# Written order, half-row loads and a bounded softmax around the attention stages of a four-layer kernel

## Chip, cores and metric

The kernel runs on one core of a Trainium2 chip as one launch. The metric is the time of one execution on the device in microseconds (us), lower is better. Three runs of the kernel before gave 7562.25, 7568.02 and 7576.92 us, with a median of 7568.02 us. About 0.2% (15 us) is the smallest difference that such runs can tell from none.

## What is computed

The reference takes 8 images of 56 x 56 places with 128 channels through four layers, all in float32. Layers 0 (a deformable convolution) and 1 (a whitening of channels) are not touched. Layers 2 and 3, on the 3136 tokens t of an image, are

```python
# layer 2
h = (layernorm(t) @ W_k.T) in 8 heads of 16
t = t + softmax(h h.T / 4) h @ W_o.T          # h is query, key and value
t = t + experts(layernorm(t))
# layer 3
q, k, v = (layernorm(t) @ w_in.T) in 4 heads of 32
q = softmax(q over the 32 of a head) / sqrt(32)
k = softmax(k over all 3136 tokens)
t = t + layernorm(((k.T v / 3136) applied to q) @ w_out.T + b_out) * ln_w
t = t + experts(layernorm(t))
```

`experts` takes the logits of 64 experts for every token and a softmax over the tokens; each expert takes its 8 best tokens of an image, sums them with their weights, passes the sum through a two-layer network, and adds the result back to those tokens.

## The kernel before

Layer 2 begins in `attention_keys` (L1038), image by image. Two loads bring the image (`y` in device memory) as the tile `t`, 112 tokens on the partitions and 28 groups on the free axis; 28 pairs of `bn_stats` and `bn_aggr` on DVE (L1066, L1067) give mean and variance; `rsqrt` (L1135) takes the power -1/2 of all 28 at once on POOL (L1140); 28 normalisations on DVE write `xn` (in `normalize`, L112); TensorE transposes each (L121) and ACT copies four at a time to `xT` (L122). From `xT` come the keys, 14 products `p_h` of 448 columns (L1082), whose results go to `kT` by turns on DVE (L1090) and ACT (L1086), and the values, 25 pairs `p_v` (L1097), copied to `va` by turns on ACT (L1105) and DVE (L1107). `kT` and `va` are stored to device memory. POOL squares the image's `va` (L1116), DVE sums the squares by head (L1118) and takes the largest (L1119). After the last image a bound `low` of all scores follows from that. In this function the order of instructions on each engine is chosen when the kernel is built, by a scheduler that follows the program's order where it has no reason to leave it. `query_bound` (L2079) then takes a bound `low3` of layer 3's queries from the rows of `w_in`, with a flag `small3` that is 1 while the bound is below 40.

`attend` (L1154) is the main part: for each image, half of its heads and block of up to 384 queries (9 blocks) it makes scores (L1251), takes exponentials (L1259) and multiplies by the values (L1304). A finished block is divided, projected (L1374) and added to its tokens (L1385), normalised (L1390 to L1399), transposed (L1411) and given its expert logits `pr` (L1415, L1416). These finishing steps are a generator that `later` holds; at the end of the program two of those that are left go on at a time. The last image's choice of tokens (`choose`, L1654: largest 8, L1659; their places, L1662; gathers, L1726; exponentials, L1693; sum, L1721) follows.

`context_sums` (L1947) is the first part of layer 3. Of each of 56 groups of 448 tokens it takes statistics (L2018, L2019), power (L1140), `ms` (L2026), normalisation on ACT (L2033), transposition to `xT`, which is stored too, and the keys `p_k` with channels on the partitions (L1980). As the softmax over tokens needs a bound that is not known, it carries a running maximum: DVE takes each group's maximum (L1983, L1985), ACT the exponential with it (L1992) and the factor `fall` by which the earlier sums shrink (L1987); the exponentials are transposed (L1997), copied (L1998), multiplied with the tokens (L2002), and DVE adds to `tot` and `den` (L2004, L2005). `linear_layer` (L2106) is the second part. A group passes ten steps, one per turn of `pipeline` (L1934), which starts a group each turn and lets every group in flight go one step, oldest first: load `xT`; `p_q` (L2131) and exponential (L2144); sum, reciprocal, `q*m` on POOL (L2148); transposition of q; `p_y` (L2155), squares on ACT (L2161), `rs` (L2165, L2166); `y` on DVE (L2169) and `t = t + y` on POOL (L2172); statistics; `ms` and `xn`, with two stores of t (L2181); transposition; `p_g` (L2187) and `pr` (L2188). After an image's seventh group `choose` follows in the same turns. Here too the scheduler decides the order in the end. Groups hold three buffers of most tiles, and images two of `t`.

Of the kernel before, what the change touches and what calls it, by code (L numbers as in the profile page):

```python
# [8 lines left out]
F32 = mybir.dt.float32  # L9
I32 = mybir.dt.int32  # L10
# [1027 lines left out]
def attention_keys(tc, k, w, yv, tok, kT_out, va_out, low, small):  # L1038
# [5 lines left out]
    n_b = yv.shape[1]  # L1044
    with ExitStack() as ctx:
        cp = ctx.enter_context(tc.tile_pool(name="akc", bufs=1))
        bp = ctx.enter_context(tc.tile_pool(name="akb", bufs=2))
        ps = ctx.enter_context(tc.tile_pool(name="akp", bufs=6, space=PSUM))
        vas = []
# [8 lines left out]
        for n in range(n_b):  # L1058
            t_sb = bp.tile([T, NT, C], F32, name="t")
            for h in range(2):  # L1060
                nc.sync.dma_start(t_sb[h * IW : (h + 1) * IW], yv[h, n])
            nc.sync.dma_start(tok[n].rearrange("(t p) c -> p t c", p=T), t_sb)
# [53 lines left out]
            nc.gpsimd.tensor_tensor(sq, v, v, ALU.mult)  # L1116
            top = bp.tile([128, 2 * KT * 4], F32, name="top")
            nc.vector.tensor_reduce(top, sq, AX.X, ALU.add)  # L1118
            nc.vector.tensor_reduce(tops[:, n : n + 1], top, AX.X, ALU.max)  # L1119
# [1267 lines left out]
```

## Time and profile before

| what | us |
|---|---|
| median of three runs | 7568.02 |
| the profiled execution, its time | 7568.32 |
| its span | 7566.5 |
| layers 0 and 1, and the weights of layers 2 and 3 | to 1520 |
| `attention_keys` and `query_bound` | 1520.06 to 1867.6 |
| `attend`, main part | 1868.9 to 6411 |
| `attend`, last blocks | 6411 to 6455.0 |
| last choice, experts of layer 2 | 6455.0 to 6663.6 |
| `context_sums` | 6670.0 to 6909 |
| `context_weights` | to 6915.0 |
| `linear_layer`, first `p_q` to last `p_g` | 6926.7 to 7323.7 |
| last choice, experts of layer 3 | 7323.7 to 7566.5 |

The profiled execution took 1.8 us more than its span, and 0.3 us more than the median of the runs. The rows are read off the timeline: the first and last instruction of each function's lines. A line of the timeline has the start, the duration, the engine, the line of the kernel, the operation, what it writes and reads with shapes, how many were merged, and in brackets the idle time ahead of it with what ended it. PE is the matrix unit, PEld its weight loads, DVE the vector engine, ACT the scalar engine, POOL GpSimd, and SP the engine that starts the transfers.

### The profile page before, as it was taken

What the parts mean: (1) busy time and instruction counts of PE and PEld (TensorE: products, weight loads), DVE (VectorE), ACT (ScalarE), POOL (GpSimd) and SP (SyncE); (2) the same over time, 40 slices, a digit from 0 to 9 for tenths busy, and PEclk for the clock granted to TensorE, in tenths of its full rate; (3) what the DMA queues carried; (4) which work ended last, traced back from release to release, by engine and by line L of the source; (5) the groups of instructions that cost most, each with busy time, mean ns of one, the idle gap of its engine ahead of it and who ended that gap; (6) DMA issues with size and microseconds to landing.
All of it is one profiled execution on the core that took longest, in us unless ns stands there. A gap on an engine that the chain in (4) does not pass through costs nothing. (4 is left out here: it accounts for less than half of the span.)

```text
span 7566.5 us, 158564 instructions
## 1 busy us (share of the span) xinstructions
PE 6499.5 (86%) x60063; PEld 2893.4 (38%) x60063; DVE 5210.3 (69%) x9787; ACT 4198.0 (55%) x6563; POOL 2941.4 (39%) x2557
## 2 busy tenths in 40 slices
PE   7859999656999999999999999999999999556764
PEld 5646666433333323323323323323333323245542
DVE  7866664366677777777777777777777777356761
ACT  5634444222766666666666666666666665156750
POOL 0011111122544444444444444444444444333763
PEclk9968989866999999999999999999999999789776
DMA  6544343476888778778778778778778777544544
GB/s 162 163 101 88 85 87 63 155 224 202 198 202 205 188 187 205 190 185 205 192 186 205 189 185 206 187 189 205 191 186 206 187 185 170 202 109 125 134 132 139
DMA packets 737876, 1287.44 MB, mean 170 GB/s; under 512 B 119042, under 2 KB 504452, under 8 KB 730308
## 3 DMA queue, kind: packets, MB, share of 16 engines
q1 hardware_dynamic: 726868, 1260.77, 65.9%
q0 software_dynamic: 6144, 12.60, 0.6%
q8 instruction: 486, 7.96, 0.5%
q10 hardware_dynamic: 4080, 3.68, 0.2%
q14 instruction: 298, 2.44, 0.1%
HBM read 286.04 MB, written 197.81 MB: 64 GB/s over the span
## 5 line engine op out<-in xcount | busy, mean ns | idle before, releaser
L1259 ACT ACTIVATE e<-p_s 128x768 f32<-128x768 f32 (+2 forms) x3712 | 2887.7, 830 | 1577.2 <-PE p_s L1251 1312.7
L1297 POOL COPY x<-sq 32x1152 f32<-32x1152 f32 x1792 | 2062.4, 1151 | 2008.8 <-PE p_s L1251 1240.1
L1270 DVE STREAM_TRANSPOSE sq<-e 128x768 f32<-128x768 f32 x2688 | 2433.8, 950 | 516.7 <-ACT e L1259 267.0
L1251 PE MATMUL p_s<-q,kT 32*128 32x384 f32 (+2 forms) x14848 | 1893.4, 547 | 41.1 <-ACT e L1259 23.3
L1304 PE MATMUL av<-e,va 128*32 128x384 f32 (+2 forms) x14848 | 1644.2, 515 | 13.5 <-DVE acc L1327 8.5
L1304 PE MATMUL avx<-x,va 128*32 128x384 f32 x10752 | 1129.5, 492 | 57.5 <-issue 36.9
L1251 PEld LDWEIGHTS p_s<-q,kT 32*128 32x128 f32 (+1 forms) x14848 | 649.9, 180 | 1265.8 <-issue 836.1
L1304 PEld LDWEIGHTS av<-e,va 128*32 128x32 f32 (+1 forms) x14848 | 293.6, 108 | 1028.7 <-issue 938.6
L1304 PEld LDWEIGHTS avx<-x,va 128*32 128x32 f32 x10752 | 351.8, 111 | 635.8 <-issue 597.4
L616 POOL TENSOR_TENSOR rs<-rs,mhalf 112x4 f32<-112x4 f32 x112 | 116.0, 1036 | 786.2 <-DVE rs L615 786.2
L1323 DVE TENSOR_TENSOR acc<-acc,avx 128x384 f32<-128x384 f32 x336 | 183.7, 547 | 232.3 <-PE avx L1304 227.7
L121 PE MATMUL p_tr<-ident,xn 112*128 112x112 f32 x672 | 132.9, 337 | 184.0 <-DVE xn L112 138.3
L1140 POOL TENSOR_TENSOR rs<-rs,mhalf 112x4 f32<-112x4 f32 (+2 forms) x136 | 167.9, 1235 | 243.6 <-DVE ntop L1985 123.9
L532 ACT COPY wT<-p_w 88x448 f32<-88x448 f32 x152 | 138.1, 923 | 197.8 <-PE p_w L530 159.4
L2033 ACT ACTIVATE xn<-t,ms,rs 112x128 f32<-112x128 f32 x448 | 185.2, 487 | 73.8 <-DVE ms L2026 73.7
L644 PE MATMUL p_f<-x1T,w 128*128 128x448 f32 x448 | 206.1, 584 | 4.4 <-DVE x1T L639 2.8
L121 PEld LDWEIGHTS p_tr<-ident,xn 112*128 112x128 f32 x672 | 97.3, 167 | 278.2 <-issue 184.9
L530 PE MATMUL p_w<-ident,wide 112*88 112x112 f32 x896 | 144.6, 300 | 62.7 <-DMA px<-strips 37.8
L1393 POOL TENSOR_TENSOR rs_b<-rs_b,mhalf 128x3 f32<-128x3 f32 (+1 forms) x72 | 58.5, 815 | 352.8 <-DVE rs_b L1392 350.2
L327 DVE SCALAR_TENSOR_TENSOR acc<-xp,dw,acc 128x3136 f32<-128x3136 f32 x48 | 166.5, 3470 | 37.6 <-ACT acc L322 37.3
L628 DVE TENSOR_TENSOR y<-y,p_rs 128x448 f32<-128x448 f32 x112 | 69.2, 618 | 176.7 <-PE p_rs L621 176.6
L122 ACT COPY xT<-p_tr 128x448 f32<-128x448 f32 x112 | 59.6, 532 | 224.8 <-PE p_tr L121 198.7
(366 smaller groups left out, 7904.0 us busy)
## 6 DMA issues: line engine op xcount, KB each, us to landing
x<-sq SPq DMA_DIRECT2D x5376, 144.0 KB
w<-in_L_ffn_weight_dram SPq DMA_DIRECT2D x64, 1024.0 KB
px<-strips SPq DMA_DIRECT2D x64, 616.0 KB
va_d<-va SPq DMA_DIRECT2D x16, 1600.0 KB
xT_d<-xT SPq DMA_DIRECT2D x112, 224.0 KB
xT<-xT_d SPq DMA_DIRECT2D x112, 224.0 KB
kT_d<-kT SPq DMA_DIRECT2D x16, 1568.0 KB
t<-t_a SPq DMA_DIRECT2D x16, 1568.0 KB
```

The source lines that it names most:

```text
L121: nc.tensor.transpose(p[:, i, :], src[:, i, :], k.ident[:T, :T])
L327: nc.vector.scalar_tensor_tensor(acc, xp[:, j // 3 : j // 3 + IH, j % 3 : j % 3 + IW], dw[:, j : j + 1], acc, ALU.mult, ALU.add,)
L530: nc.tensor.transpose(p[:, g], around[:, :, g], k.ident[:T, :T])
L644: nc.tensor.matmul(p, q.w1[:, f * 128 : (f + 1) * 128], x1T, start=True, stop=True)
L1140: nc.gpsimd.tensor_tensor(rs, rs, k.mhalf[:m, :n], ALU.pow)
L1251: nc.tensor.matmul(ss[j // 2][:m, j % 2, :width], kT[rows, 128 * i : 128 * i + m], q[rows, :width], start=True, stop=True,)
L1259: nc.scalar.activation(e[:m, 2 * j : 2 * j + 2, :width], ss[j][:m, :, :width], AF.Exp)
L1270: nc.vector.transpose(sq[:, :, i, j : j + 2].rearrange("p s j c -> p j s c"), exps[u, b, a, i][:, j : j + 2, :QB].rearrange("p j (s c) -> ...
L1297: nc.gpsimd.tensor_copy(*moves.pop(0))
L1304: nc.tensor.matmul(out, keys[u, b][1][:m, i, j, :], e[j], start=start, stop=stop)
L1323: nc.vector.tensor_tensor(to, to, in_order(av), ALU.add)
L2033: nc.scalar.activation(out[:, i], x[:, i], AF.Identity, bias=ms[:, i : i + 1], scale=rs[:, i : i + 1])
```

## The change

In five places:

- `attention_keys` runs under `manual_schedule`: each engine gets its instructions in the order in which the program writes them. The loads of an image are taken by half rows, so that a partition reads 28 tokens that lie together (14336 bytes) where it read single tokens of 512 bytes; the token stores are alike. The tokens of a transposed group are then 28 apart, and ACT's copy puts them in place with a stride. Statistics and power of image n+1 are written between the key products of image n. All 14 key results go through ACT. The square of image n stays on POOL after its values, and DVE's two reductions of it come after the normalisation of image n+1.
- The last blocks of `attend` all go on together, from before the last jobs, with their `t` and `xT` in two buffers that the exponentials no longer need.
- `query_bound` becomes `score_bound`: it takes the rows of keys too, and stands at the head of the token layers.
- `context_sums_bounded` is new and is taken where `small3` is 1, `context_sums` otherwise. It has no maximum and no rescaling: `low3` stands in for the maximum, the keys come out with tokens on the partitions, so that the exponentials need no transposition, and one accumulator in PSUM runs over all 56 groups; a column of ones beside the tokens gives the denominator. It is under `manual_schedule`.
- `linear_layer` is under `manual_schedule`, with no operation changed.

```diff
-def attention_keys(tc, k, w, yv, tok, kT_out, va_out, low, small):
+def attention_keys(tc, k, w, y, tok, kT_out, va_out, low, small):
...
+        ctx.enter_context(
+            tc.manual_schedule(
+                engines={
+                    e.engine for e in (nc.tensor, nc.scalar, nc.vector, nc.gpsimd, nc.sync)
+                }
+            )
+        )
...
+        def statistics(n):
...
             t_sb = bp.tile([T, NT, C], F32, name="t")
-            for h in range(2):
-                nc.sync.dma_start(t_sb[h * IW : (h + 1) * IW], yv[h, n])
-            nc.sync.dma_start(tok[n].rearrange("(t p) c -> p t c", p=T), t_sb)
+            inner = tok[n].rearrange("(h f i) c -> f h i c", f=2, i=NT)
+            for f in range(2):
+                of = slice(f * IH, (f + 1) * IH)
+                nc.sync.dma_start(t_sb[of], y[:, n, f * NT : (f + 1) * NT])
+            yield
+            for f in range(2):
+                nc.sync.dma_start(inner[f], t_sb[f * IH : (f + 1) * IH])
             mv = bp.tile([T, NT, 2], F32, name="mv")
             st = bp.tile([T, NT, 6], F32, name="st")
             for i in range(NT):
                 nc.vector.bn_stats(st[:, i], t_sb[:, i])
                 nc.vector.bn_aggr(mv[:, i], st[:, i])
-            rs = rsqrt(nc, k, bp, mv, NT)
+                if i % GT == GT - 1:
+                    yield
+            stats[n] = t_sb, mv, rsqrt(nc, k, bp, mv, NT)
...
+        def largest(n):
...
+            sq = bp.tile([128, 2 * KT * 4, DK], F32, name="sq", bufs=1)
+            v = vas[n % 2].rearrange("p g t j d -> p (g t j) d")[:, :, :DK]
+            nc.gpsimd.tensor_tensor(sq, v, v, ALU.mult)
+            yield
+            top = bp.tile([128, 2 * KT * 4], F32, name="top")
+            nc.vector.tensor_reduce(top, sq, AX.X, ALU.add)
+            nc.vector.tensor_reduce(tops[:, n : n + 1], top, AX.X, ALU.max)
+        stats, tail = {}, []
+        ahead = [statistics(0)]
+        while ahead:
+            advance(ahead)
+        for n in range(n_b):
+            t_sb, mv, rs = stats.pop(n)
+            if n + 1 < n_b:
+                ahead.append(statistics(n + 1))
+                advance(ahead)
             xT = bp.tile([C, S], F32, name="xT")
+            by_place = xT.rearrange("c (h f i) -> c i f h", f=2, i=NT)
             for g in range(NG):
                 xn = bp.tile([T, GT, C], F32, name="xn")
                 for i in range(GT):
                     normalize(nc, xn[:, i], t_sb[:, g * GT + i], mv, rs, g * GT + i)
-                transpose_group(
-                    nc, k, ps, "m", xT[:, g * QC : (g + 1) * QC], xn, nc.scalar.copy
-                )
-            kT = bp.tile([128, 2, S], F32, name="kT", bufs=1)
+                p = ps.tile([C, GT, 2, IH], F32, tag="m", name="p_tr")
+                for i in range(GT):
+                    nc.tensor.transpose(
+                        p[:, i].rearrange("c f h -> c (f h)"), xn[:, i], k.ident[:T, :T]
+                    )
+                nc.scalar.copy(by_place[:, g * GT : (g + 1) * GT], p)
+            advance(tail)
+            kT = bp.tile([128, 2, S], F32, name="kT")
             for g in range(2):
...
                         p, wk[:, g * 128 : (g + 1) * 128], xT[:, cols], start=True, stop=True
                     )
-                    if c % 2:
-                        nc.scalar.activation(
-                            kT[:, g, cols], p, AF.Identity, bias=w.one16, scale=DK**-0.25
-                        )
-                    else:
-                        nc.vector.tensor_scalar(
-                            kT[:, g, cols], p, DK**-0.25, w.one16, ALU.mult, ALU.add
-                        )
+                    advance(ahead)
+                    nc.scalar.activation(
+                        kT[:, g, cols], p, AF.Identity, bias=w.one16, scale=DK**-0.25
+                    )
                 nc.sync.dma_start(kT_out[n, g], kT[:, g])
+            assert not ahead
             va = vas[n % 2]
             for t, m in key_tiles():
                 p = ps.tile([128, 2, 4, DK], F32, tag="m", name="p_v")
@@ -1107,16 +1148,10 @@
                     nc.vector.tensor_copy(va[:m, :, t, :, :DK], p[:m])
             for g in range(2):
                 nc.sync.dma_start(va_out[n, g], va[:, g].rearrange("p t j d -> p (t j d)"))
-            sq = bp.tile([128, 2 * KT * 4, DK], F32, name="sq", bufs=1)
-            v = va.rearrange("p g t j d -> p (g t j) d")[:, :, :DK]
-            nc.gpsimd.tensor_tensor(sq, v, v, ALU.mult)
-            top = bp.tile([128, 2 * KT * 4], F32, name="top")
-            nc.vector.tensor_reduce(top, sq, AX.X, ALU.add)
-            nc.vector.tensor_reduce(tops[:, n : n + 1], top, AX.X, ALU.max)
+            tail.append(largest(n))
+            advance(tail)
+        while tail:
+            advance(tail)
...
-            t_sb = wp.tile([128, KB + 1, C], F32, name="t", bufs=2)
+            if ending:
+                t_sb = rooms[0].pop().rearrange("p (a c) -> p a c", c=C)
+            else:
+                t_sb = wp.tile([128, KB + 1, C], F32, name="t", bufs=2)
...
-            st = wp.tile([128, KB + 1, 6], F32, name="st", bufs=2)
-            mv = wp.tile([128, KB + 1, 2], F32, name="mv", bufs=2)
-            rs = wp.tile([128, KB + 1], F32, name="rs_b", bufs=2)
+            st = wp.tile([128, KB + 1, 6], F32, name="st", bufs=NQ)
+            mv = wp.tile([128, KB + 1, 2], F32, name="mv", bufs=NQ)
+            rs = wp.tile([128, KB + 1], F32, name="rs_b", bufs=NQ)
...
-            xT = wp.tile([C, QB + 64], F32, name="xT", bufs=2)
+            if len(rooms) == 2:
+                xT = rooms[1].pop()
+            else:
+                xT = wp.tile([C, QB + 64], F32, name="xT", bufs=2)
...
+        def room():
+            flat = tp.tile([128, 4, KB, 4, KB * 32], F32, name="sq")
+            flat = flat.rearrange("p s a j c -> p (s a j c)")
+            return [flat[:, 512 * i : 512 * i + 512] for i in range(NQ)]
...
+        def go_on_all():
...
+        ending = True
+        rooms = [room()]
+        early = 3
         while jobs:
             keep_squares()
+            if early:
+                go_on_all()
+                early -= 1
             from_squares()
-        for work in urgent:
-            go_on(work)
-        ending = True
+            while urgent:
+                go_on(urgent.pop(0))
+        while urgent:
+            go_on(urgent.pop(0))
+        rooms.append(room())
         while later:
-            for work in later[:2]:
-                go_on(work)
+            go_on_all()
...
+def context_sums_bounded(tc, k, w, low, t_in, xT_out, tot, den):
...
+        bp = ctx.enter_context(tc.tile_pool(name="cbb", bufs=3))
+        wp = ctx.enter_context(tc.tile_pool(name="cbw", bufs=3))
+        ps = ctx.enter_context(tc.tile_pool(name="cbp", bufs=7, space=PSUM))
+        pa = ctx.enter_context(tc.tile_pool(name="cba", bufs=1, space=PSUM))
...
+        sums = pa.tile([C, C + 1], F32, name="sums")
...
+        def load():
...
+        def group(n, g):
+            if g == 0:
+                load()
...
+            rs, mv = group_stats(nc, k, wp, t)
+            yield
+            ms = minus_mean(nc, wp, rs, mv)
+            xn = wp.tile([T, GT, C + 1], F32, name="xn", bufs=6)
+            nc.gpsimd.memset(xn[:, :, C:], 1.0)
+            for i in range(GT):
+                if i % 2:
+                    nc.scalar.activation(
+                        xn[:, i, :C],
+                        t[:, i],
+                        AF.Identity,
+                        bias=ms[:, i : i + 1],
+                        scale=rs[:, i : i + 1],
+                    )
+                else:
+                    nc.vector.tensor_scalar(
+                        xn[:, i, :C],
+                        t[:, i],
+                        rs[:, i : i + 1],
+                        ms[:, i : i + 1],
+                        ALU.mult,
+                        ALU.add,
+                    )
+            yield
+            p = ps.tile([C, GT, T], F32, tag="m", name="p_tr")
+            for i in range(GT):
+                nc.tensor.transpose(p[:, i], xn[:, i, :C], k.ident[:T, :T])
+            xT = wp.tile([C, QC], F32, name="xT")
+            nc.scalar.copy(xT, p.rearrange("c a t -> c (a t)"))
+            nc.sync.dma_start(xT_out[n][:, g * QC : (g + 1) * QC], xT)
+            yield
+            p = ps.tile([T, GT, C], F32, tag="m", name="p_k")
+            for i in range(GT):
+                nc.tensor.matmul(
+                    p[:, i],
+                    xT[:, i * T : (i + 1) * T],
+                    w.w_in[:, C : 2 * C],
+                    start=True,
+                    stop=True,
+                )
+            e = wp.tile([T, GT, C], F32, name="e")
+            nc.scalar.activation(e, p, AF.Exp, bias=low[:T])
+            yield
+            for i in range(GT):
+                nc.tensor.matmul(
+                    sums,
+                    e[:, i],
+                    xn[:, i],
+                    start=(n == 0 and g == 0 and i == 0),
+                    stop=(n == n_b - 1 and g == NG - 1 and i == GT - 1),
+                )
+        load()
+        load()
+        pipeline([group(n, g) for n in range(n_b) for g in range(NG)], 1)
+        nc.vector.tensor_copy(tot, sums[:, :C])
+        nc.vector.tensor_copy(den, sums[:, C:])
...
-def query_bound(tc, k, w, w_in, low, small):
+def score_bound(tc, k, w_in, low, small):
...
-        raw = bp.tile([C, C], F32, name="raw")
-        nc.sync.dma_start(raw, w_in[:C])
-        sq = bp.tile([C, C], F32, name="sq")
+        raw = bp.tile([C, 2, C], F32, name="raw")
+        nc.sync.dma_start(raw, w_in[: 2 * C].rearrange("(a p) c -> p a c", p=C))
+        sq = bp.tile([C, 2, C], F32, name="sq")
         nc.vector.tensor_tensor(sq, raw, raw, ALU.mult)
+        norms = bp.tile([C, 2], F32, name="norms")
+        nc.vector.tensor_reduce(norms, sq, AX.X, ALU.add)
         norm = bp.tile([C, 1], F32, name="norm")
-        nc.vector.tensor_reduce(norm, sq, AX.X, ALU.add)
+        nc.vector.tensor_reduce(norm, norms, AX.X, ALU.max)
...
         bp = ctx.enter_context(tc.tile_pool(name="llb", bufs=2))
         wp = ctx.enter_context(tc.tile_pool(name="llw", bufs=3))
...
+        ctx.enter_context(
+            tc.manual_schedule(
+                engines={
+                    e.engine for e in (nc.tensor, nc.scalar, nc.vector, nc.gpsimd, nc.sync)
+                }
+            )
+        )
...
+        low3 = cp.tile([128, 1], F32, name="low3")
+        small3 = cp.tile([1, 1], I32, name="small3")
+        score_bound(tc, k, a["L3_attn_w_in"], low3, small3)
...
+            attention_keys(tc, k, w, y, tok, kT_d, va_d, low, small)
...
-        low3 = cp.tile([128, 1], F32, name="low3")
-        small3 = cp.tile([1, 1], I32, name="small3")
-        query_bound(tc, k, w, a["L3_attn_w_in"], low3, small3)
...
-        context_sums(tc, k, w, t_a, xT_d, tot, den)
+        sums = (t_a, xT_d, tot, den)
+        taken = nc.values_load(small3[0:1, 0:1], min_val=0, max_val=1)
+        with tc.If(taken > 0) as both:
+            context_sums_bounded(tc, k, w, low3, *sums)
+        with both.Else():
+            context_sums(tc, k, w, *sums)
```

More of the change, by code (lines that the diff above doesn't have):

```diff
@@ L1035, in key_tiles @@
     return [(t, min(128, S - 128 * t)) for t in range(KT)]
-def attention_keys(tc, k, w, yv, tok, kT_out, va_out, low, small):
+def attention_keys(tc, k, w, y, tok, kT_out, va_out, low, small):
     nc = tc.nc
-    n_b = yv.shape[1]
+    n_b = y.shape[1]
     with ExitStack() as ctx:
@@ L1057, in attention_keys @@
         wk = w.wk.rearrange("p h d -> p (h d)")
-        for n in range(n_b):
+        def statistics(n):
             t_sb = bp.tile([T, NT, C], F32, name="t")
-            for h in range(2):
-                nc.sync.dma_start(t_sb[h * IW : (h + 1) * IW], yv[h, n])
-            nc.sync.dma_start(tok[n].rearrange("(t p) c -> p t c", p=T), t_sb)
+            inner = tok[n].rearrange("(h f i) c -> f h i c", f=2, i=NT)
[5 more added lines that the diff above has]
+                nc.sync.dma_start(inner[f], t_sb[f * IH : (f + 1) * IH])
             mv = bp.tile([T, NT, 2], F32, name="mv")
@@ L1428, in go_on @@
                 later.remove(work)
-        ready, ending = [], False
+        ready, ending, rooms = [], False, []
         loads = [(u, b) for u in range(1, len(parts)) for b in (8, 7, 3, 2, 1, 6, 5, 4, 0)]
@@ L1488, in attend @@
             reload()
+        def room():
[3 more added lines that the diff above has]
+        def go_on_all():
+            for work in list(later):
+                if work not in urgent:
+                    go_on(work)
+        ending = True
+        rooms = [room()]
+        early = 3
         while jobs:
             keep_squares()
+            if early:
+                go_on_all()
+                early -= 1
             from_squares()
-        for work in urgent:
-            go_on(work)
-        ending = True
+            while urgent:
[3 more added lines that the diff above has]
+        rooms.append(room())
         while later:
-            for work in later[:2]:
-                go_on(work)
+            go_on_all()
 def attend_any(tc, k, w, yv, kT_in, va_in, t_out, gate_w, gate_b, taken, pooled, t_g):
@@ L2010, in context_sums @@
         pipeline([group(n, g) for n in range(n_b) for g in range(NG)], 1)
+def context_sums_bounded(tc, k, w, low, t_in, xT_out, tot, den):
+    nc = tc.nc
+    n_b = len(t_in)
+    with ExitStack() as ctx:
+        bp = ctx.enter_context(tc.tile_pool(name="cbb", bufs=3))
[10 more added lines that the diff above has]
+        sums = pa.tile([C, C + 1], F32, name="sums")
+        loaded = []
+        def load():
+            if len(loaded) < n_b:
+                t = bp.tile([T, NT, C], F32, name="t")
+                load_tokens(nc, t, t_in[len(loaded)])
+                loaded.append(t)
+        def group(n, g):
+            if g == 0:
+                load()
+            t = loaded[n][:, g * GT : (g + 1) * GT]
+            rs, mv = group_stats(nc, k, wp, t)
[54 more added lines that the diff above has]
+        nc.vector.tensor_copy(den, sums[:, C:])
@@ L2115, in linear_layer @@
         ps = ctx.enter_context(tc.tile_pool(name="llp", bufs=8, space=PSUM))
+        ctx.enter_context(
+            tc.manual_schedule(
+                engines={
+                    e.engine for e in (nc.tensor, nc.scalar, nc.vector, nc.gpsimd, nc.sync)
+                }
+            )
+        )
         st_of = {}
@@ L2277, in token_layers @@
             small = cp.tile([1, 1], I32, name="small")
-            attention_keys(tc, k, w, yv, tok, kT_d, va_d, low, small)
+            attention_keys(tc, k, w, y, tok, kT_d, va_d, low, small)
         pooled = [cp.tile([C, n_b, E], F32, name=f"pooled{i}") for i in range(2)]
-        low3 = cp.tile([128, 1], F32, name="low3")
-        small3 = cp.tile([1, 1], I32, name="small3")
-        query_bound(tc, k, w, a["L3_attn_w_in"], low3, small3)
         dest = (t_a, *gates[0], choices[0], pooled[0])
```

## Prediction

> **What bounds the kernel now.** I read the timeline first for the stages, then the busy times of each stage (columns: window, length, then busy us and instructions of PE, PEld, DVE, ACT, POOL, PE's granted clock, the transfers' share, GB/s).
>
> ```profile
> 1520.00:1868.00 348.00, 200.79 (x854) 133.25 (x854) 234.20 (x877) 85.69 (x200) 83.05 (x17) 0.71 0.68 218
> 1868.00:6411.00 4543.00, 4373.10 (x41604) 1432.35 (x41605) 3427.70 (x4913) 2922.92 (x3818) 2150.02 (x1894) 0.98 0.80 194
> 6411.00:6475.00 64.00, 25.70 (x101) 16.65 (x100) 36.70 (x104) 5.52 (x15) 9.30 (x11) 0.60 0.11 33
> 6670.00:6909.00 239.00, 169.90 (x1008) 122.92 (x1008) 172.00 (x840) 167.47 (x448) 56.40 (x56) 0.95 0.34 96
> 6927.00:7324.00 397.00, 281.40 (x1560) 207.18 (x1559) 305.10 (x1132) 297.64 (x1000) 275.01 (x259) 0.80 0.51 132
> ```
>
> The main part of `attend` is PE's, 4373 of 4543 us; the change leaves it alone. In the four other rows no engine is busy for over 77%: they are bound by chains from engine to engine, and the change acts only there. The chain of image 2 in the keys, from the timeline:
>
> ```profile
> 1605.89 4.79 POOL L1140 TENSOR_TENSOR rs<-rs,mhalf 112x28 f32<-112x28 f32 x1 [4.82 <-DVE rs L1139]
> 1610.72 7.27 DVE L112 TENSOR_SCALAR xn<-t,mv,rs 112x128 f32<-112x128 f32 x28 [4.91 <-POOL rs L1140]
> ...
> 1630.41 5.88 PE L1097 MATMUL p_v<-wkT,xT 128*128 128x128 f32 x50
> ...
> 1636.78 5.52 POOL L1116 TENSOR_TENSOR sq<-va 128x3200 f32<-128x3200 f32 x1 [26.09 <-DVE va L1107]
> 1642.33 3.48 DVE L1118 TENSOR_REDUCE top<-sq 128x200 f32<-128x3200 f32 x1 [2.85 <-POOL sq L1116]
> ```
>
> An image takes 41.2 us (the next normalisations begin at 1651.9), and PE works only from 1611.2 to 1636.3: the rest is square, reductions, statistics and power, one after another. The next pairs show two engines in each other's way in `linear_layer`:
>
> ```profile
> 7036.91 1.07 DVE L1705 TENSOR_SCALAR found<-found,tot 64x8 f32<-64x8 f32 x1
> 7036.91 1.05 POOL L2148 TENSOR_TENSOR q<-q,m 112x512 f32<-112x512 f32 x1 [0.33 <-ACT q L2144]
> ...
> 7052.43 2.17 DVE L112 TENSOR_SCALAR chosen<-chosen,cmv,rs 128x128 f32<-128x128 f32 x4
> 7052.49 1.26 POOL L2172 TENSOR_TENSOR t<-t,y 112x512 f32<-112x512 f32 x1
> ```
>
> Eight elements took DVE 1.07 us, as long as POOL's product. Of the four normalisations (median 0.335) the first began before POOL's sum, yet the four took 2.17: POOL got in between two of them, and one then lasted 1.40, till POOL was done. Last, `context_sums`: POOL's power is held behind DVE's maximum, and DVE behind the power.
>
> ```profile
> POOL rs L1140 <- DVE ntop L1985: 123.9, 41, 3.5
> ...
> DVE ms L2026 <- POOL rs L1140: 48.7, 48, 1.4
> ```
>
> **What the Trainium skill says.** "SBUF — State Buffer", section Who interferes with whom: DVE and GpSimd share a pair of ports under an exclusive lock; a DVE instruction with two SBUF inputs, or a `tensor_scalar` in its two-port mode, blocks for the whole of a GpSimd instruction that reads SBUF, whichever comes second. The trace agrees: the pairs above, and `ms`, 0.162 us at the median in `context_sums` and 0.857 in `linear_layer`. "DMA: Bandwidth & Descriptors", section Specifications, gives 512 bytes as enough for the line rate. The trace doesn't: with the transfers' share near full, the `kT` and `va` stores move 350 to 487 GB/s, and the loads of y, in 512-byte packets, 126 to 179. The measurement decides. Its section Issuing engines are not separate DMA queues says that all transfers share 16 engines: a load waits behind the stores ahead of it. "TensorE: Matmul & The Clock Gate", Part 1, puts an idle PE at half clock; here the clock is 0.50 from 1610.7 to 1617.6, after 16 us of idling, and 1.00 in the values.
>
> **Part 1, keys (1520.06 to 1867.6, 347.5 us).** First load: 12 us from 1508.0 to its use; at the stores' rate 1.6 MB take 4 us, but DVE has the weights until 1515.7 (`score_bound`'s few operations there too), so first statistics near 1516.5: -3.5. Then 12.6 us to the first normalisation, as before (1520.1 to 1532.7): 1529.1. First image: 28 normalisations 7.3, last transposition and strided copy 1.7 (nearest row: the strided 88x448 copy of L532, 0.923 us, against 0.532 for L122), `p_h` 28 x 0.375 = 10.5 and 0.5 at low clock, `p_v` 5.9: 25.9, to 1555.0. All key copies on ACT: 14 x 0.63 = 8.8, under `p_h`'s 11. Statistics (7.5 us) and power (4.8) of n+1 lie beside `p_h` and `p_v`, the reductions (3.9) ahead of them: 13 + 3.9 + 7.5 + 4.8 = 29.2 us after the image's start. The load of n+1 waits behind two stores of `va`, 3.3 MB, 8 us, lands near 13, in time; with the cover gone it would push the power. But POOL's square of n now meets the normalisation of n+1. Both become free at the last `va` copy; DVE gets one in, POOL enters behind it, as at 7052, and the other 27 wait 5.5 us. PE and ACT have nothing else. So each of seven further images takes 25.9 + 5.5 = 31.4: 1774.8. At the end square 5.7, reductions 3.8, the `low` chain 2.6 as before: 1786.9. `query_bound` no longer follows. Saved: 80.7, say 80. Bounds: 118 if DVE keeps the ports and POOL waits (7 x 5.5 more); 60 if load or power is late by 3 us an image.
>
> **Part 2, last blocks of `attend`.** From 6410.9 to 6455.0, 44 us, five blocks go as 2, 2, 1, rounds of 15.1 us (additions at 6417.5, 6432.5, 6447.6), with DVE idle for more than half. A block costs DVE 0.55 + 1.36 + 0.17 + 0.86 + 0.56 + 0.61 = 4.1 us. In lockstep one latency of about 15 remains, and the other blocks' work fills its gaps; two of the blocks start before the last jobs. With some 14 us of DVE after 6413.5 and 4 of waits it ends at about 6432: -22. Bounds 12 (the early blocks delay the last jobs) and 28.
>
> **Part 3, `context_sums_bounded` (239 us).** The rows of `w_in` have a largest squared norm of 1.43, so the bound is sqrt(1.01 x 128 x 1.43) = 13.6, under 40, and the new branch runs. Gone per group: maximum 0.61, `ntop` 0.15, `fall` 0.29, transposition of exponentials 1.07, copy 0.68, `tot` 0.32, `den` 0.20. PE is left with the sums 1.07 (`p_x`'s row), keys 1.04 (`p_q`'s, the same shape) and transpositions 0.55 = 2.7; ACT with two `xn` 0.82, copy 0.53, exponential 0.70 = 2.05. But the written order on DVE is `ms`, two `xn`, statistics of the next group, `rs`, and `ms` waits for the power of that `rs`: 1.3 (power 1.01, two semaphores) + 0.16 + 0.55 + 1.3 = 3.3 us. 56 x 3.3 + 12 to fill = 197 against 239, and the first statistics no longer stand behind a DVE write that waited for the last scatter, 4 us: -42 with a little given back for stores behind 1.6 MB loads. Bounds: 80 (PE's 2.7), 4 (as slow as the 4.25 now).
>
> **Part 4, `linear_layer` (397 us, 49.7 per image).** A clear turn takes 5.37 us now (the sums on POOL at 6961.78, 6967.15, 6972.52), in a loop of POOL and DVE: the power `rs` waits for `q*m`, `y` for that power. So 7 x 5.37 = 37.6, and `choose` adds 12.1. In the written order POOL takes power, sum, power, product, each ready when its turn comes; ACT becomes the longest, 4.47 (6962.86 to 6967.33 without a gap), with crossings 4.7: 32.9 per image. The price is `choose`, which comes first in its turn and now holds an engine's head. DVE's largest 8 (3.4) delay `ms` and so ACT's `xn`: +3.3. The places (3.4), with the statistics of the previous image's choice ahead of them, hold ACT at `found`: +5.9. The copy of `pooled` waits for PE on DVE: +3.3. Four gathers on POOL, 1.25 each, push `q*m`: +1.1. Seven exponentials on ACT: +4.7. Sum 18.3, image 51.2: +12 in all. SP runs a turn or more ahead, so the load of t (9 us at the slow rate) makes `p_q` late by some 2 us in the turn in which ACT waits for DVE anyway. Bounds: -49 (4.5 and 12.1 as now), +64 (5.1 and 22). `score_bound`'s move: 0 to 3, hidden by the first load.
>
> **Sum.** -80 - 22 - 42 + 12 = -132 on the profiled execution's 7568.3 (span 7566.5 and 1.8 around it; 0.3 over the median): 7436.
>
> **Rivals.**
> (a) *No collision in the keys.* DVE holds the ports through its 28 normalisations and POOL's square follows. The first begins first (at the `va` copy's end; POOL came 0.17 us after it); the four normalisations at 7052 speak against. 7436 - 38 = 7398.
> (b) *`choose` costs more in the written order.* Several engines' heads wait in one turn, 24 us per image: 7436 + 46 = 7482.
> (c) *`context_sums_bounded` reaches PE's pace*, if statistics slip beside the power: 7436 - 34 = 7402.
> (d) *Slower than before.* Each choice empties the pipeline of ten turns, since gathers wait for stores of the same turn and everything stands behind them: a refill of 9 x 4.7 = 42 us and 18 on top, 8 x 42 = +336 on the layer: 7772. It turns the sign from 17 us per image over my figure. Against it: SP's stores go out a turn and more ahead of the gathers.
>
> **Chances.** Forecast 0.57, (a) 0.17, (b) 0.13, (c) 0.09, (d) 0.04. The forecast's own bounds by half give 7395 to 7480; with (a), (b) and (c) the range is 7375 to 7495. About 0.2% is what a measurement can tell from none. Faster 0.95, within 0.2% 0.01, slower 0.04.
>
> **What would show it.** Keys: a period of 31.4 us, one normalisation of about 5.5 us beside each square, PE idle for 6 us ahead of the transpositions. Last blocks: five additions in a row, `choose` 22 us earlier. Sums: a period of 3.3 with DVE's `ms` waiting for POOL. Linear layer: clear turns of 4.7, 18 us more around each choice, ACT waiting for DVE at `found`. I am wrong if the keys' period is 26, if a turn stays at 5.4, or if POOL stands before the gathers for stores.

## The result, and the profile after

Six runs of each kernel gave a median of 7502.58 us after (7495.93 to 7534.45) against 7572.47 us before (7562.25 to 7587.27). The ratio is 0.9913 with a 95% interval from 0.9891 to 0.9935: about 66 us (49 to 83) faster, half of the 132 that were forecast. The profiled execution took 7496.52 us with a span of 7494.4, 72.1 us less than the span before. Both timelines, cut at the same instructions, say where they are:

| from, to | before | after | change | forecast |
|---|---|---|---|---|
| start, first scores `p_s` of `attend` | 1878.2 | 1820.1 | -58.1 | -80 |
| first, last `p_s` | 4517.1 | 4521.2 | +4.1 | 0 |
| last `p_s`, last `pr` of `attend` | 59.1 | 37.7 | -21.4 | -22 |
| last `pr`, first statistics of the sums | 215.6 | 214.5 | -1.1 | -4 |
| first statistics, `tot` | 238.9 | 225.2 | -13.7 | -38 |
| `tot`, first `p_q` | 17.8 | 19.6 | +1.8 | 0 |
| first `p_q`, last `p_g` | 397.0 | 412.2 | +15.2 | +12 |
| last `p_g`, end | 242.8 | 243.9 | +1.1 | 0 |

Of the first row's 58.1 us, 6.2 lie ahead of the keys' first statistics (1520.1 before, 1513.9 after; 3.5 were forecast), and 52.1 behind. In the profiles of the experiments below, whose edits leave everything ahead of it alone, that moment lies anywhere between 1509.3 and 1522.0; so the gains of the keys are counted below from the first statistics.

The busy times of the stages after, with the columns as in the prediction:

```profile
1513.00:1810.00 297.00, 211.43 (x853) 137.29 (x852) 235.80 (x809) 151.09 (x264) 82.34 (x16) 0.77 0.73 256
1820.00:6361.00 4541.00, 4380.84 (x41636) 1437.21 (x41639) 3438.31 (x4935) 2922.84 (x3818) 2151.93 (x1896) 0.98 0.79 193
6361.00:6404.00 43.00, 15.85 (x73) 9.98 (x65) 29.12 (x84) 6.80 (x16) 10.15 (x10) 0.66 0.18 55
6593.00:6819.00 226.00, 153.94 (x1120) 132.50 (x1120) 134.68 (x674) 106.69 (x225) 59.46 (x112) 0.96 0.38 107
6838.00:7250.00 412.00, 276.49 (x1559) 198.14 (x1560) 314.92 (x1119) 291.69 (x1000) 272.34 (x258) 0.80 0.48 126
```

In the sums PE, DVE and ACT all have less to do than before, 154, 135 and 107 us against 170, 172 and 167, and yet the stage is only 14 us shorter: no engine is busy for over 70% of it. So again a chain holds it. In the keys DVE has as much to do as before, 236 us.

The keys of image 2 (counted from 0) on the timeline after:

```profile
1589.65 4.79 POOL L1175 TENSOR_TENSOR rs<-rs,mhalf 112x28 f32<-112x28 f32 x1 [24.60 <-DVE rs L1174]
1594.41 5.52 POOL L1093 TENSOR_TENSOR sq<-va 128x3200 f32<-128x3200 f32 x1
1594.48 5.53 DVE L112 TENSOR_SCALAR xn<-t,mv,rs 112x128 f32<-112x128 f32 x1 [0.87 <-POOL rs L1175]
1594.48 12.45 DVE L112 TENSOR_SCALAR xn<-t,mv,rs 112x128 f32<-112x128 f32 x28 [0.87 <-POOL rs L1175]
```

The last two lines are one stretch, the first normalisation alone and then all 28. The collision is there: one of them lasts as long as POOL's square, and the 28 take 12.45 us where they took 7.27. But the period is 34.1 us (the mean between the powers from 1589.65 to 1760.23), not 31.4, and the normalisation waits 0.87 us for the power, which I had put well ahead of it. Before, the same mean was 43.5: I had written 41.2, but the normalisations that follow those of image 2 begin at 1654.21, not at 1651.9.

The rest of an image is longer than forecast too. First the granted clock when `p_h` begins, before and after (the clock is the third number from the end of a line):

```profile
1617.60:1621.60 4.00, 4.00 (x9) 2.18 (x9) 1.07 (x3) 1.14 (x3) 0.00 (x0) 0.50 0.06 14
1573.40:1578.00 4.60, 4.60 (x7) 2.26 (x8) 2.16 (x2) 1.27 (x2) 0.00 (x0) 0.53 0.87 240
```

At that clock the products of `p_h` start 0.75 us apart instead of 0.375. From the first `p_h` to the first `p_v` it was 12.8 us in image 2 before, and after it is 12.8 in the first two images and 12.2 to 12.4 in the others; I had 11.0. Then `p_v`, in image 3 and in the last image after:

```profile
1657.95 3.76 PE L1138 MATMUL p_v<-wkT,xT 128*128 128x128 f32 x30 [0.35 <-ACT va L1146]
...
1791.41 5.88 PE L1138 MATMUL p_v<-wkT,xT 128*128 128x128 f32 x50
```

The 50 products took 5.88 us in every image before and take 6.9 to 7.1 after, with PE waiting for ACT's copies in the middle; only in the last image they take 5.88. So an image in the middle is 14.0 us from its first normalisation to `p_h`, 12.3 to `p_v`, 6.9 to the end of `p_v` and 0.9 to the next normalisation.

Two views tell what makes the power late. The first is of the statistics, one image of before and then one of after:

```profile
1525.22 0.26 DVE L1066 BATCH_NORM_STATS2 st<-t 112x6 f32<-112x128 f32 x1
1525.40 0.17 DVE L1067 BATCH_NORM_AGGREGATE mv<-st 112x2 f32<-112x6 f32 x1
1525.48 0.26 DVE L1066 BATCH_NORM_STATS2 st<-t 112x6 f32<-112x128 f32 x1
```

```profile
1578.58 0.26 DVE L1081 BATCH_NORM_STATS2 st<-t 112x6 f32<-112x128 f32 x1
1578.87 0.18 DVE L1082 BATCH_NORM_AGGREGATE mv<-st 112x2 f32<-112x6 f32 x1
1578.97 0.26 DVE L1081 BATCH_NORM_STATS2 st<-t 112x6 f32<-112x128 f32 x1
```

A pair takes 0.26 us before and 0.39 after, with the same two durations. From the start of a `bn_stats` to the next `bn_aggr` it was 0.18 us and is now 0.29. Both orders alternate the two, but the image of before begins with two `bn_stats` and ends with two `bn_aggr`, so that there the next `bn_stats` lies between a `bn_aggr` and the one that it reads. The second view is of the transfers, in slices of 0.5 us from 1560 to 1580, before and after:

```profile
GB/s 410 410 410 307 461 435 435 410 410 410 410 410 410 77 333 22 210 309 189 173 157 178 160 135 71 2 0 0 0 33 0 0 0 0 0 0 0 0 0 0
```

```profile
GB/s 410 410 410 410 410 410 410 410 410 410 410 410 410 410 410 230 179 258 401 201 201 172 172 201 172 229 258 229 172 172 147 258 115 401 344 287 401 201 315 258
```

The 410 are stores of keys and values, from 128 partitions. The load behind them runs at 135 to 190 before and for the most part at 150 to 260 after, though its packets are then 14336 bytes long; towards the end stores of `tok` run beside it. The Trainium skill, "SBUF — State Buffer", section Door 1: The DMA port swizzle, says that bandwidth goes with the ports which a transfer's partitions reach, that partitions 0 to 63 reach 8 of the 16, and gives 196 GB/s for 64 partitions against 328 for 128. Each half of this load covers 56 partitions, before and after, and its rate is near that figure. No run here loads over more partitions at once, so that their number is the cause is not shown; shown is that packets 28 times as long did not bring the stores' rate. I had taken the stores' rate, and had read the short packets as the cause.

In the sums the same pairs lie on the loop between DVE and POOL:

```profile
6702.57 0.16 DVE L2174 SCALAR_TENSOR_TENSOR ms<-mv,rs 112x4 f32<-112x4 f32 x1 [1.19 <-POOL rs L1175]
...
6703.36 0.29 DVE L2166 BATCH_NORM_STATS2 st<-t 112x6 f32<-112x128 f32 x1
...
6705.15 0.17 DVE L1174 TENSOR_SCALAR rs<-mv 112x4 f32<-112x4 f32 x1
...
6705.47 1.01 POOL L1175 TENSOR_TENSOR rs<-rs,mhalf 112x4 f32<-112x4 f32 x1 [2.88 <-DVE rs L1174]
...
6706.51 0.16 DVE L2174 SCALAR_TENSOR_TENSOR ms<-mv,rs 112x4 f32<-112x4 f32 x1 [1.19 <-POOL rs L1175]
```

From `ms` to the statistics 0.79 us, from there to `rs` 1.79, to the power 0.32, to the next `ms` 1.04: 3.94 us, the period. The term that I had at 1.3 is 1.79.

In the last blocks the five additions lie within 16.3 us, from 6354.12 to 6370.42, where before three rounds lay 15 us apart (6417.5 to 6447.6). The third and the last:

```profile
6360.68 0.52 DVE L1423 TENSOR_TENSOR sq<-sq,p_s 128x384 f32<-128x384 f32 x1
...
6370.42 0.55 DVE L1423 TENSOR_TENSOR sq<-sq,p_s 128x384 f32<-128x384 f32 x1
```

In the linear layer a turn without a step of the choice takes 4.4 or 5.1 us: the seven turns of the first image, which no choice disturbs, take 33.5 us, 4.8 each, and took 36.6 before. In the other turns the engines wait for the choice. The timeline of POOL and the waits of the stage:

```profile
7024.94 1.26 POOL L2329 TENSOR_TENSOR t<-t,y 112x512 f32<-112x512 f32 x1
...
7029.35 1.26 POOL L2329 TENSOR_TENSOR t<-t,y 112x512 f32<-112x512 f32 x1
```

```profile
PE p_pool L1780 <- DVE chosen L112: 48.6, 11, 8.8
...
ACT found L1726 <- DVE ntop L1723: 40.0, 7, 6.6
```

`found` waited 14.6 us in all for DVE before, and waits 40.0 now. The seven turns of an image, between the sums on POOL from 7012.93 on, are 12.0, 4.4, 5.1, 5.6, 7.2, 7.7 and 10.9: 52.9 us. The five images from 6926.9 on take 53.6 on the mean, against 51.2 forecast and 49.2 before.

### The profile page after: what moved, and what is told of

Same layout as the page of the kernel before. It is cut to its first block, busy times and chain, and to the rows that moved or that the text cites. A ratio compares the mean times of both kernels' runs of the same rounds, so it can differ in the third digit from the quotient of the medians.

```text
span 7494.4 us, 158624 instructions
## 1 busy us (share of the span) xinstructions
PE 6489.8 (87%) x60175; PEld 2897.8 (39%) x60175; DVE 5187.6 (69%) x9559; ACT 4196.3 (56%) x6404; POOL 2942.3 (39%) x2613
## 5 line engine op out<-in xcount | busy, mean ns | idle before, releaser
L649 PE MATMUL p_f<-hid,w 128*128 128x448 f32 x448 | 181.6, 549 | 0.0
L645 ACT ACTIVATE hid<-p_f,b 128x448 f32<-128x448 f32 x224 | 136.8, 638 | 55.4 <-PE p_f L644 47.8
L530 PEld LDWEIGHTS p_w<-ident,wide 112*88 112x88 f32 x896 | 119.6, 172 | 108.9 <-issue 75.1
L1360 DVE COPY acc<-avx 128x384 f32<-128x384 f32 x112 | 61.6, 550 | 142.0 <-PE avx L1339 142.0
```

Of the source, the lines that this page charges most:

```text
L530: nc.tensor.transpose(p[:, g], around[:, :, g], k.ident[:T, :T])
L649: nc.tensor.matmul(p[:, :QC], q.w2[:, f], hid[:, f], start=(f == 0), stop=(f == 3))
```

## Experiments

All are edits of the kernel after. Most of them ran once, so they are judged by the stages of one profile. Whole times are no measure there: first `p_s` to last `avx` of `attend`, which no edit but that of the last blocks touches, took between 4528 and 4564 us in these profiles (4532 before, 4541 after). Periods of the keys are means of the five between the third and the eighth power; those of the sums are medians.

**Pairs apart.** All `bn_stats` of a group ahead of its `bn_aggr`, in `group_stats`, shown here, and in the keys:

```diff
     for i in range(GT):
         nc.vector.bn_stats(st[:, i], x[:, i])
+    for i in range(GT):
         nc.vector.bn_aggr(mv[:, i], st[:, i])
```

> All four bn_stats of a group are written ahead of its four bn_aggr, in the keys, the sums and the linear layer; nothing else changes. Theory (a bn_aggr written right behind its own bn_stats makes DVE wait 0.13 us for the result, which the scheduler of before had spread out): a pair goes from 0.39 to 0.26 us; the sums' period from 3.94 to about 3.43, 28 us off that stage (225 to 197); the keys' statistics from 11.0 to 7.3 us per image, but their period only from 34.2 to about 33.2, since PE's own chain remains, 7 us; the linear layer within 5. Some 35 us in all. Rival (the pairs are not on the path, the crossings to POOL and back are): the sums stay at 3.9, the whole within 5 us.

In the sums a group's statistics look so:

```profile
6700.60 0.87 DVE L2167 BATCH_NORM_STATS2 st<-t 112x6 f32<-112x128 f32 x4
...
6701.38 0.36 DVE L2169 BATCH_NORM_AGGREGATE mv<-st 112x2 f32<-112x6 f32 x4
```

Four pairs and the way to `rs` took 1.25 us, not 1.79, and the period fell to 3.39 us. From first `ms` to `tot` the stage took 192.3 us, 29.8 less than after (222.1). That is the expected size, and the rival is out: the pairs were on the path of the sums. In the keys the period stayed at 34.1, so there I was 1 us off. The power was in time, for POOL now waited 3.3 us for the values ahead of each square, but the granted clock stayed low for 4.6 us of `p_h` instead of 3.4, and `p_h` took 12.9 us instead of 12.3. The linear layer took 412.1 us as after: there the pairs are off the path.

**Square after the normalisation.** POOL first copies a column that ACT has just written:

```diff
-            advance(tail)
+            if tail:
+                mark = bp.tile([C, 1], F32, name="mark")
+                nc.gpsimd.tensor_copy(mark, xT[:, S - 1 : S])
+                advance(tail)
+                advance(tail)
...
             tail.append(largest(n))
-            advance(tail)
```

With the last line gone, `largest(n)` no longer begins right behind its own image's values.

> POOL copies one column of image n+1's last transposed group ahead of the square of image n, so that the square starts when the normalisation is over. Theory (two chains of equal length in the keys: PE's with the collision, 34.3 us, and store of va, load, statistics, power, 17.6 + 11.1 + 4.8 = 33.5 us): the 28 normalisations go from 12.5 back to 7.3 us, yet the period stays between 33.3 and 34.3, so at most 7 us are won. Rival (the collision alone sets the period): the period falls to about 28.8 and 38 us are won.

The chain of one image:

```profile
1628.85 6.04 PE L1142 MATMUL p_v<-wkT,xT 128*128 128x128 f32 x28 [6.12 <-DVE va L1152]
...
1635.14 7.26 DVE L112 TENSOR_SCALAR xn<-t,mv,rs 112x128 f32<-112x128 f32 x28
```

The normalisations are back at 7.26 us: it was the square that held them. The period is no shorter, it is longer, 36.5 us. The reductions now wait for the later square, the statistics stand behind them on DVE, and the copies of the values stand behind the statistics; PE waits 6.12 us in the middle of the values. So the rival is out, and the second chain is a little longer than I thought, for the written order puts the copies of `va` on it.

**Early load.** Image n+2 is loaded right after image n's normalisation, and image 1 right behind image 0.

```diff
...
+            if n + 2 < n_b:
+                loads.append(statistics(n + 2))
+                advance(loads)
             kT = bp.tile([128, 2, S], F32, name="kT")
```

> As after, but the load of image n+2 is started right after the normalisation of image n, not after the stores of image n's values. Theory (two chains of about 34 us each): the load is no longer late, statistics end before the values begin, the wait of p_v for DVE's copies goes; the period is left to PE's chain with the collision, 12.5 + 1.6 + 12.9 + 5.9 = 32.9; 6 to 9 us won in the keys. Rival (the late load is the only limit): the period falls to below 31, over 22 us won.

The period was 34.3 us: neither number. The sum was wrong in `p_v`: with the collision an image is 14.1 us from its first normalisation to `p_h`, 13.0 for `p_h`, 6.9 for `p_v`, not 5.9, and 0.2 to the next normalisation: 34.2, and neither load nor power is waited for. So PE's chain with the collision alone gives the period of the kernel after, and the other chain is as long.

**Early load and pairs apart, with the collision.** The edits of pairs apart and of the early load together.

> Pairs apart and early load as in e6, but the square of image n stays where after has it, beside the normalisation of n+1. Theory (with the second chain short, the collision is the limit): the period is 33.3 to 34.3 us, against 30.5 in e6, so the collision costs 3 to 4 us per image on top of what is late next. Rival (the collision is hidden by another wait): 30.5 as in e6.

The period was 34.3 us. With the square moved too it is 31.0 (next). The collision costs 3.3 us per image over what is late next, some 23 us for seven images. The last experiment, which moves square and reductions, comes to 28.7: 5.6 us less than with the collision, about the 5.5 that the forecast had charged for it.

**All three in the keys.** The edits of pairs apart, late square and early load together.

> In the keys all three at once: pairs apart (in the sums and the linear layer too), the square of image n after the normalisation of n+1, and the early load. Theory: with the collision gone and the second chain shortened, PE's chain is left, 7.3 + 1.6 + 12.9 + 5.9 = 27.7; a period of 27.7 to 29, 37 to 45 us off the keys against after, though the late square alone won nothing. Rival (PE's half clock or the transfers hold an image at 33 or more): at most 8 us. The sums fall by the 29 us of the separate pairs as well.

The period was 31.0 us. From the first statistics to the first `p_s` it was 277.1 us, 29.0 less than after (306.1): most of it, not all. The sums fell by 29.8. What is late next in the keys:

```profile
1626.96 3.49 DVE L1097 TENSOR_REDUCE top<-sq 128x200 f32<-128x3200 f32 x1 [7.27 <-POOL sq L1094]
...
1643.22 7.28 DVE L112 TENSOR_SCALAR xn<-t,mv,rs 112x128 f32<-112x128 f32 x28 [0.78 <-POOL rs L1184]
```

DVE waits 7.27 us for the late square with the statistics behind it, and so the next normalisation waits for the power.

**Layer 3's sums, one turn more.** A second `yield` between statistics and `ms`:

```diff
             rs, mv = group_stats(nc, k, wp, t)
             yield
+            yield
             ms = minus_mean(nc, wp, rs, mv)
```

> In context_sums_bounded one more turn lies between a group's statistics and its ms, so that the power has a turn of its own. Theory (the loop of statistics, power and ms through DVE and POOL sets the 3.94 us): the period falls to DVE's own work, 0.27 + 0.52 + 1.79 + 0.17 = 2.75, or PE's 2.7: some 2.8 us, 64 us off the stage (225 to 161). Rival (the stores of xT behind the loads, or DVE's dependent pairs alone, hold it): it stays above 3.5.

From first `ms` to `tot` it took 186.8 us, 35 less than after and not 64. Most turns took 2.9 us, so the rival is out, but some took 4 to 6. The waits show that the longer pipeline had too few buffers:

```profile
DVE rs L1174 <- ACT xn L2110: 32.8, 38, 3.5
...
ACT xT L2131 <- DMA xT_d<-xT: 11.8, 5, 3.0
```

**The same with five buffers and pairs apart.**

```diff
-        wp = ctx.enter_context(tc.tile_pool(name="cbw", bufs=3))
+        wp = ctx.enter_context(tc.tile_pool(name="cbw", bufs=5))
```

> context_sums_bounded with one more turn between statistics and ms, five buffers where it had three, and pairs apart. In e4 DVE waited for ACT's normalisations to free a buffer of rs (32.8 us) and ACT for stores of xT (11.8). Theory: with buffers for the longer pipeline the period falls to DVE's or PE's own work, 2.3 to 2.8 us; from first ms to last sum 222 us become 150 to 163. Rival (something else than DVE, POOL and buffers holds the turn): above 180, as e4.

169.2 us, a period of 2.93, 53 us less than after. The rival is out; 6 us are missing to my range. PE is busy for 106 of 130 us at full clock there, and DVE still waits 0.9 us for ACT in most groups; the reason for that wait is open.

**The linear layer left to the scheduler.**

```diff
-        ctx.enter_context(
-            tc.manual_schedule(
...
         st_of = {}
```

> linear_layer without its manual schedule, all else as after. Theory (the written order costs that layer 15 us, through choose at the heads of the engines): first p_q to last p_g goes from 412 back to 397, all else stays, 15 us off the whole. Rival (the 15 us come from elsewhere, such as transfers or the granted clock): it stays at 412.

First `p_q` to last `p_g` took 397.3 us: 15 less, as before the change, and an image in the middle 49.2. The written order is the cause of the loss.

**Choice at the end of a turn.** In the written order, the steps of `choose` come last in a turn and not first:

```diff
-                yield from choose(nc, k, wp, ps, pr, t_out[n], taken[:, n], pooled[:, n])
+                chosen.append(choose(nc, k, wp, ps, pr, t_out[n], taken[:, n], pooled[:, n]))
...
+            advance(flight, len(flight))
+            advance(chosen, going)
```

> As after, with the manual schedule of the linear layer, but the steps of choose are written at the end of a turn and not at its head. Theory (the 15 us of the linear layer are stalls of ACT, DVE and POOL behind the steps of choose at their heads): 412 us from first p_q to last p_g fall to 395 to 404, since the engines then wait for each other with one turn's work already given out. Rival (it is the work of choose in any fixed place that costs, or the clear turn is no shorter than before): 408 or more.

407.2 us: between the two, and nearer to the rival. The five images in the middle take 52.7 us on the mean, 0.9 less than after and 3.5 more than with the scheduler. So standing at the head is only a small part of the cost. That the rest comes from the fixed place itself, where the other engines wait while one of them does a step of the choice, fits the waits but was not tested apart.

**Last blocks not early.**

```diff
-        early = 3
+        early = 0
```

> As after, but the last blocks of attend begin to go on together only when the last jobs are over (early = 0). Theory (the early blocks hold DVE while the last jobs wait for it): from last p_s to last avx 19.7 us go back to 15.0, and from last avx to last pr 18.6 us become 24 to 28, so that the early start is worth 1 to 4 us. Rival (the 4.7 us come from something else, such as the granted clock): 19.7 stay.

Last `p_s` to last `avx` took 14.7 us (19.7 after, 15.0 before), last `avx` to last `pr` 23.8 (18.0 after, 44.1 before). So the early start does hold the last jobs by 5 us, and gives 5.8 back: it is worth 0.8 us, too little to tell from nothing in one profile, and nearly the whole gain comes from the lockstep.

**Everything.** Pairs, late square and early load in the keys, sums with one more turn and five buffers, linear layer scheduled:

> All of it: the three edits of the keys, the sums with one more turn and five buffers, the linear layer left to the scheduler. Theory: against after 40 us in the keys, 62 in the sums, 15 in the linear layer, together some 117: about 7385, 0.975 of before. Rival (gains that are lost again further on): under 80 of them arrive.

Five runs had a median of 7409.65 us, 0.9782 of before (0.9767 to 0.9798), 25 us short of the expected time. Against the median after that is 93 us, so the rival is out. In its profile the keys gave 29 us against after, counted from the first statistics, the sums 53 and the linear layer 18.

**And the reductions behind the statistics.** The second step of `largest` moves (against the version before this one):

```diff
                 nc.gpsimd.tensor_copy(mark, xT[:, S - 1 : S])
                 advance(tail)
-                advance(tail)
...
             assert not ahead
+            advance(tail)
```

> As e7, and the two reductions of image n's squares are written behind the statistics of image n+2 instead of ahead of them. Theory (in e6 the late square pushes reductions, statistics and power, so that the normalisation waits 0.8 us and the values' copies too): statistics end 4 us earlier, PE's chain alone is left, 7.3 + 1.6 + 13 + 6.9 = 28.8; the period falls from 30.5 to about 29, 10 us off the keys against e7; about 7398, 0.977 of before. Rival (PE's half clock in p_h holds the image): the period stays at 30.5 and the time that of e7.

```profile
1636.69 7.25 DVE L112 TENSOR_SCALAR xn<-t,mv,rs 112x128 f32<-112x128 f32 x28
...
1651.33 3.48 DVE L1097 TENSOR_REDUCE top<-sq 128x200 f32<-128x3200 f32 x1
1651.50 4.80 POOL L1184 TENSOR_TENSOR rs<-rs,mhalf 112x28 f32<-112x28 f32 x1 [0.31 <-DVE rs L1183]
```

The statistics end at 1651.2, ahead of the reduction, and the power ends 9 us before the next normalisation begins (1665.14). The period was 28.7 us, and from the first statistics to the first `p_s` it was 263.5 us, 43 less than after and 14 less than in the version before this one. The images now take 28.5 and 29.6 us by turns, as the clock stays low for 3.8 or 6.0 us of `p_h`, which then takes 12.5 or 13.6. Five runs had a median of 7390.76 us, 0.976 of before (0.9737 to 0.9782). It is the fastest version; its interval overlaps that of the one before, so in the whole time the last step is not shown, only in the keys.

## Why the prediction was right and wrong

- *What bounds the kernel* held: chains from engine to engine, with `attend`'s main part untouched. Its 4 us of loss lie within the 36 us by which that part differs between the profiles.
- *Part 1, the keys.* The collision of square and normalisation came as priced: one normalisation of 5.5 us, 12.45 for the 28. Only the order was another. From image 2 on the square began first, by 0.07 us, as POOL goes to it straight from the late power, and it was the first normalisation that lasted 5.53. (In the pair from 7052 that the forecast leans on, the 1.40 us are those of the first normalisation too.)

  The step that failed is the rest of the period, put at 25.9 us. Its term for `p_h`, 10.5 "and 0.5 at low clock", was too small: 12.2 to 12.8, since the clock stays at half for the first 3.2 to 4.5 us. The trace of before has it in the same place, 12.8 us for image 2, so it could have been read there. `p_v` took 6.9 to 7.1 instead of 5.9. Its cause is open: ACT has the same keys to write in the last image, where `p_v` takes 5.88, and with the early load it is 6.9 though DVE copies in time. And 0.9 us pass until the next normalisation, with the power late, where I had none. That is some 2.7 us in each of eight images (34.1 for 31.4, and 29.0 for 25.9 in the first), 21 of the part's shortfall of 22.

  "Lands near 13, in time" failed as well: the load landed 18.9 us after the image's start and the statistics took 11.2 us, not 7.5. By itself that costs little in the kernel after; it is the second chain of equal length, which took most of what single edits of the keys could have won. The result lies near the bound of 60, but by luck: that stood for a late load or power, and with the load early the period stayed at 34.3.
- *Part 2* held: -21.4 against -22. The early start, which I had counted in, gave 0.8 at most.
- *Part 3* failed in one term of the 3.3 us, which was too small: statistics 1.3 us, read from a trace in which the scheduler had put other work between the two instructions of a pair. In the written order it is 1.79. With the pairs apart the stage fell by 29.8 us, more than the 24 that were missing: the 12 us to fill the pipeline, on the other side of my sum, were 5 (225.2 less 56 x 3.94). The rest of the 3.94 is 0.79 where I had 0.71 and 1.36 where I had 1.3. The 4 us of an earlier start came out as 1.1. The bound, PE's 2.7, was nearly reached: 2.93, but not in this order. The loop that I had named was the right one.
- *Part 4* held in sum, +15.2 against +12: clear turns of 4.8 us on the mean where I had 4.7, and 20 us for the choice (53.6 less seven such turns) instead of 18. The reason "at the head" is borne out only in small part: at the end of a turn an image costs 0.9 us less, of 4.4 lost.
- *Rivals.* (a) is out by the trace; (c) came near only with one more turn and more buffers; (b), with 24 us for the choice, and (d) did not come. None was the cause of the miss, which lay in two durations: the statistics, taken from another order, and `p_h`, taken at another clock.

The span of before plus the four parts as measured is 7566.5 - 58.1 - 21.4 - 14.8 + 15.2 and 7 us of small changes: 7494.4, the span.

## What to carry to other kernels

A duration read from a trace belongs to the order in which it was taken: when an order is to be written by hand, take each instruction's start-to-start time with its own producer right ahead of it, or write the independent ones side by side. It belongs to its clock too: where PE has paused ahead of a stretch of products, take the whole stretch from the trace and not the spacing at full clock. A pipeline that hides one wait needs a look at the next chain before a gain is promised: here two chains of 34 us stood side by side, and only the edits together won. Before a transfer is priced, look at the rate of one over the same partitions.

## What the runs showed of the hardware

- `bn_aggr` written right behind the `bn_stats` that it reads costs 0.13 us more per pair than with another `bn_stats` between, or with four of each in a row (0.39 against 0.26).
- A load over 56 partitions ran at 135 to 190 GB/s with packets of 512 bytes and at 150 to 260 with packets of 14336 bytes; the stores from 128 partitions ran at 410.
- POOL's square of 5.52 us held up a run of DVE normalisations in every image of the kernel after but the first: the first of the run, where the square had begun 0.07 us earlier, and the second (5.60 us) in image 1, where the square began 0.22 us later. A power of four values for each partition, 1.01 us, did not: in the kernel before three normalisations from 7053.75 on ran beside one at 0.33 us each.
- How long `p_h` took followed how long the granted clock stayed at half after it began: 12.3 us with 3.4, 12.9 with 4.6, 13.6 with 6.0 (after, pairs apart, last experiment), each time 10.6 us and half of that time.
